# In a step whose product begins a half, the piece goes ahead of the product; the first transposition of x moves one step later

## The chip, the cores and the metric

The kernel runs on one core of a Trainium2 chip. The metric is the device time of one execution in microseconds (us); lower is better. The core has five engines that work side by side: PE (TensorE, matrix products, results into the accumulation memory PSUM), DVE (VectorE), ACT (ScalarE), POOL (GpSimd) and SP (SyncE, which here only issues transfers). Each engine takes its own instructions in the order of its own queue and waits on semaphores for what others have to finish first.

## What is computed

The input is x with 16 graphs of 1024 nodes and 128 features, and one adjacency matrix of 1024 by 1024 for all of them. Three transformer layers with 8 heads of 16 features, masked by the adjacency, are followed by one graph attention layer. Cut to what matters (`ln` is the layer norm):

```
for l in 0, 1, 2:
    Q, K, V = x @ Wq, x @ Wk, x @ Wv                      # 8 heads of 16
    scores  = where(adj == 0, -inf, Q K^T / 4)            # 1024 x 1024 a head
    x = ln(x + softmax(scores) V @ Wo + bo)
    x = ln(x + relu(x @ W1 + b1) @ W2 + b2)               # 256 hidden
h   = x @ W
e   = leaky_relu(h @ a_src [:, None] + h @ a_dst [None, :], 0.2)
out = ln(softmax(where(adj == 0, -inf, e)) h + x)
```

## The kernel before

**Blocks, halves, steps.** `blocks` (L655) lists 48 pairs of a graph and a layer, four graphs at a time, so that the four take turns at layer 0, then at layer 1, then at layer 2. A block is 32 steps: two groups of four heads, two halves of 512 queries (`qh`), and eight tiles of 128 keys (`kt`). A half is one group and one `qh`, so a block has four halves of eight steps. Below, "step 12" is the step with that number within its block, and its key tile is the rest of the number divided by 8.

**A step** (the loop at L768) issues three things, and PE and ACT run them in this written order (the schedule is manual for these two at L763; the order on DVE, POOL and SP is settled by the compiling framework, which looks ahead):

- `score_step` (L415): four matmuls make the scores of four heads, two by two into two PSUM tiles `s` of two banks each. There are three such tiles (`slot`, L130). Of each pair, either ACT takes the exponential and POOL multiplies with the mask (L430, L431: only the first pair, and not where `kt` is 2, 5 or 7), or DVE adds the mask and ACT takes the exponential a little later (L433, L445).
- `av_due` (L727): the product of the step four steps earlier (`AHEAD`). `av_step` (L447) multiplies its exponentials with the values, and adds into the one accumulator `sums`, a single PSUM bank (L719). After the eighth key tile of a half, `finish` (L453) has DVE transpose the accumulator into `tt` (L461), and POOL scales it. The next half's first product overwrites `sums`, so it waits for that transposition. With four steps of delay a half's product begins at steps 4, 12, 20 and 28.
- `piece` (L691): one task of the chains of other work that stand waiting, if one is due. Nearly every piece needs the one PSUM bank `t` (`bank`, L134: `bufs=1`): its matmuls write there, and ACT or DVE copies the result out before the next piece's matmuls may write.

**Pieces.** `proj_tasks` (L357) makes the next block's projections: `t0` transposes x (twice), `split` makes K and Q as a high and a low part (four pieces: ACT writes `hi`, L385, then DVE writes `lo`, L386), `v` makes the values (two pieces, ACT copies them out, L392). `post_tasks` (L469) does what comes after the attention of the block before: `both` (transpositions on DVE), `out_proj` (two pieces, out through DVE at L329 with statistics behind it), `x1t` (two), `ffn1` (four, out through ACT at L506), `ffn2` (two). `last_tasks` (L541) is the graph attention layer of a graph: `xt`, `nodes`, `rows_gh`, `edges`, `two` (edges of one quarter and `aggregate` of the quarter before), `end`. The `edges` also need two tiles `s` and one of the six tiles `e` that the steps use.

**When a piece is due.** The table `AT` (L34) gives the step, within its block, for each of the pieces of `proj` and `post`; those of `last` keep a gap after the piece before them. Each step takes at most one piece, from the first chain that has one due. In a block without the last layer the pieces stand thus: `t0` at 3 and 6, `split` at 9, 11, 14 and 17, `v` at 19 and 20, `both` at 8 or 10, `out_proj` at 12 and 22, `x1t` at 23 and 25, `ffn1` at 26, 27, 28 and 30, `ffn2` at 0 and 8 of the block after. Twelve blocks (three groups of four) also carry the last layer of an earlier graph, and nearly every step of theirs has a piece; the last group's follows in the final block and behind it (`AT_END`, L35).

Of the kernel before, what the change touches and what calls it, by code (L numbers as in the profile page):

```python
# [30 lines left out]
FIRST = 1  # L31


AT = {"proj": (3, 6, 9, 11, 14, 17, 19, 20), "post": (12, 22, 23, 25, 26, 27, 28, 30, 32, 40, 41)}  # L34
AT_END = {3: (12, 21, 22, 24, 25, 26, 27, 28, 30, 31), 2: (8, 9, 13, 14, 15, 16, 17, 18, 20, 21)}  # L35
AHEAD = 4
BOTH_ON_DVE = (2, 5, 7)
# [78 lines left out]
def fast_path(ctx: ExitStack, tc: tile.TileContext, a: dict, out: bass.AP, flag):  # L116
# [108 lines left out]
    def first_weights():  # L225
        W[0].update(load_layer(nc, nc.sync, const, a, 0, ("Wo", "b2", "W1", "b1", "W2", "ln1_g", "ln2_g")))
        norm_weights(nc.sync, 0)
# [173 lines left out]
    def stack(m, g):  # L401

        for pp in range(2):
            for n, order in (("Wk", (0, 1, 0, 1)), ("Wq", (0, 0, 1, 1))):
                t = work.tile([P, N], F32R, tag=n, name=n, bufs=4)
                r0 = (g * J + 2 * pp) * HD
                for i, part in enumerate(order):
                    behind["stack"] = nc.sync.dma_start(t[i:P:4, :].bitcast(F32), state[n, m][part][r0:r0 + 2 * HD, :].bitcast(F32)).ins
                state[n, g, pp] = t
# [37 lines left out]
    def av_step(step, e, acc, first, last):  # L447
        m, g, qh, kt = step
        for j in range(J):
            nc.tensor.matmul(acc[j * SLOT:j * SLOT + HD + 1, :], v_bufs[m % 2][:, kt, 2 * j + g, :], e[:, j, :],  # L450
                             start=first, stop=last)

    def finish(g, qh, acc):  # L453

        def run():
            if g == 0 and qh == 0:
                state["A"] = work.tile([P, 2, 16, G, HD], F32, tag="A", name="A", bufs=1)
                state["recs"] = work.tile([P, G, 2, 16], F32, tag="recs", name="recs", bufs=2)
            tt = work.tile([P, 16, SLOT], F32, tag="tt", name="tt", bufs=1)
            with soon():  # L460
                nc.vector.transpose(tt.rearrange("p a b -> p (a b)"), acc)  # L461
            rec = state["recs"][:, g, qh, :]
            nc.vector.reciprocal(rec, tt[:, :, HD])
            nc.gpsimd.tensor_mul(state["A"][:, qh, :, g, :], tt[:, :, :HD],
                                 rec[:, :, None].to_broadcast([P, 16, HD]))
        return run
# [195 lines left out]
    def put(tasks, mark, chain=None, first=False, table=None):  # L662

        if chain is None:
            chain = {"due": now[0], "queue": deque()}
            chains.insert(0 if first else len(chains), chain)
        for n, task in enumerate(tasks):
            at = now[0] // (4 * NT) * 4 * NT + (table or AT[mark[0]])[n] if mark[0] in AT else None
            chain["queue"].append(task + (mark if n == len(tasks) - 1 else None, at))
        return chain  # L670

    def take(chain):

        _, f, tiles, mark, _ = chain["queue"][0]
        if any(free[t[1:]] == 0 for t in tiles.split() if t[0] == "+"):
            return False
        chain["queue"].popleft()
        f()
        for t in tiles.split():
            free[t[1:]] += -1 if t[0] == "+" else 1  # L680
        done.add(mark)
        chain["due"] = now[0]
        if not chain["queue"]:
            chains.remove(chain)
        return True

    def is_due(chain):
        gap, at = chain["queue"][0][0], chain["queue"][0][4]
        return now[0] >= (chain["due"] + gap if at is None else at)

    def piece():  # L691
        for chain in chains:
            if is_due(chain) and take(chain):
                return

    def need(mark):
        while mark not in done:
            first = next(c for c in chains if any(q[3] == mark for q in c["queue"]))
            assert take(first) or any(take(c) for c in list(chains) if c is not first)
# [22 lines left out]
    waiting = deque()  # L722
# [4 lines left out]
    def av_due(n):  # L727

        for item in [w for w in waiting if w[2] <= n]:
            step, e, _ = item  # L730
            half = step[:3]
            if half not in accs:
                if accs:
                    continue
                accs[half] = sums
                left[half] = NT
            waiting.remove(item)
            left[half] -= 1
            av_step(step, e, accs[half], left[half] == NT - 1, left[half] == 0)
            if left[half]:  # L740
                continue
            m, g, qh = half
            b, l = blocks[m]
            while g == 0 and qh == 0 and last_attn:
                need(last_attn.pop())
            finish(g, qh, accs.pop(half))()
            if m == len(blocks) - 1:
                if g == G - 1:
                    if qh == 0:
                        final.append(post_tasks(b, l)[1])  # L750
                    put(final[0][qh], ("final", qh), first=True)
                    if qh == 1:
                        put(last_tasks(b), ("last", b), chains[0])
            elif g == G - 1 and qh == 1:
                post = post_tasks(b, l)[0]
                chain = put(post[:1], ("attn", b, l))
                put(post[1:], ("post", b, l), chain, table=AT_END.get(len(blocks) - m))
                last_attn.append(("attn", b, l))
                if l == L - 1:
                    put(last_tasks(b), ("last", b), chain)  # L760

    n = 0
    with tc.manual_schedule(engines={mybir.EngineType.PE, mybir.EngineType.Activation}):  # L763
        for m, (b, l) in enumerate(blocks):
            order = [(g, qh) for g in range(G) for qh in range(2)]
            if m in (0, len(blocks) - 1):
                order.sort(key=lambda x: x[1])
            for at, (g, qh, kt) in enumerate((g, qh, kt) for g, qh in order for kt in range(NT)):  # L768
                now[0] = n
                if at == (6 if m == 0 else 1):  # L770
                    stack(m, 1)
                if n == 6:
                    with tc.issue_after(behind["stack"]):
                        first_weights()
                        other_weights()
                if n == 20:
                    with tc.issue_after(behind["pool"]):
                        biases()
                if n == 40:
                    with tc.issue_after(behind["dve"]):  # L780
                        last_weights()
                if at == 0 and m + 2 < len(blocks) and blocks[m + 2][1] == 0:
                    put([(0, fetch(blocks[m + 2][0]), "+x")], ("fetch", blocks[m + 2][0]))
                if m + 1 < len(blocks):
                    if at == (6 if m == 0 else 0):
                        need(("post",) + (blocks[m + 1][0], blocks[m + 1][1] - 1) if blocks[m + 1][1] else
                             ("fetch", blocks[m + 1][0]))
                        put(proj_tasks(m + 1), ("proj", m + 1), first=True)
                    if at == (24 if m == 0 else 21):
                        need(("proj", m + 1))  # L790
                        stack(m + 1, 0)
                step = m, g, qh, kt
                if FIRST <= n < FIRST + 4:

                    with tc.manual_schedule(engines={mybir.EngineType.DVE}):
                        e = score_step(step)
                        neighbours(4 + n - FIRST)
                        masks(4 + n - FIRST, mask_rows(4 + n - FIRST))
                else:
                    e = score_step(step)  # L800
                waiting.append((step, e, n + AHEAD))
                av_due(n)
                piece()
                n += 1
        exponentials(0)
        for n in range(n, n + 2 * AHEAD):
            now[0] = n
            av_due(n)
            piece()
        tail[0] = True  # L810
        while chains:
            now[0] += 1
            for chain in list(chains):
                if is_due(chain):
                    take(chain)
# [236 lines left out]
```

## Time and profile before

Median of three runs: 3982.8 us (3978.19 to 3985.26). The profiled execution took 3983.09 us, its span in the trace is 3981.2 us: 1.9 us lie around it.

| engine | busy us | share of the span |
|---|---|---|
| PE | 3758.5 | 94% |
| DVE | 3408.3 | 86% |
| ACT | 3392.8 | 85% |
| POOL | 3331.4 | 84% |
| weight loads (beside PE) | 1558.5 | 39% |

The busy time by stretch, one stretch a block, tells two kinds of blocks:

| stretch (us from the start) | what it is | length | PE busy | DVE | ACT | POOL |
|---|---|---|---|---|---|---|
| 466.0 to 539.3 | a block without the last layer | 73.3 | 70.82 | 65.33 | 69.42 | 64.73 |
| 836.1 to 931.7 | first block with it | 95.6 | 90.32 | 82.32 | 72.25 | 77.83 |
| 931.7 to 1028.7 | second | 97.0 | 90.52 | 80.97 | 72.49 | 76.88 |
| 1028.7 to 1127.5 | third | 98.8 | 91.77 | 81.42 | 73.28 | 78.53 |
| 1127.5 to 1221.1 | fourth | 93.6 | 90.84 | 79.10 | 70.85 | 75.64 |
| 1221.1 to 1294.2 | without it again | 73.1 | 70.63 | 65.08 | 69.22 | 64.58 |

To read it: PE works all but 2.5 us of 73 in the first kind and all but 3 to 7 us in the second. The other engines have some slack each, but they have it in places, not everywhere: an average of 86% can hold stretches where an engine is the last to be ready.

### The profile page before, as it was taken

Reading aid. Unit: us, or ns where it says so; the run is one execution under the profiler, and the core shown is the slowest. Engines: PE = TensorE matmul, PEld = TensorE weight load, DVE = VectorE, ACT = ScalarE, POOL = GpSimd, SP = SyncE. Lnnn points to the kernel's source line nnn. Section 1 sums busy time; section 2 is a strip of 40 time slices with the busy share of each in tenths; the row PEclk is TensorE's granted clock in tenths of the full one; section 3 lists DMA queues with packets and bytes.
Section 4 is the critical chain, followed back from the end, with each engine's and each line's share of the span. In section 5 each row is a group of like instructions: output and inputs, shape, how many; then the busy total and the mean of one; then the engine's idle time right before and its main releaser. Section 6 shows DMA issues by size and latency. Waiting matters only on the chain.

```text
span 3981.2 us, 107823 instructions
## 1 busy us (share of the span) xinstructions
PE 3758.5 (94%) x44501; PEld 1558.5 (39%) x44501; DVE 3408.3 (86%) x5326; ACT 3392.8 (85%) x3961; POOL 3331.4 (84%) x3010
## 2 busy tenths in 40 slices
PE   7999999999999999999999999999999999999996
PEld 2333333344443333334444333333444433333345
DVE  7888988988888988988888898888888898898874
ACT  7999999977779999997777999999777799999860
POOL 4788888987789888988778888888877898898875
PEclk8999999999999999999999999999999999999998
DMA  6222222112222222222222222221222212222200
GB/s 163 65 65 53 55 65 63 46 48 65 56 58 57 65 65 54 54 65 55 55 55 55 65 53 56 65 64 45 55 55 55 71 46 62 65 51 58 66 8 20
DMA packets 124465, 233.13 MB, mean 59 GB/s; under 512 B 34624, under 2 KB 73792, under 8 KB 123968
## 3 DMA queue, kind: packets, MB, share of 16 engines
q1 hardware_dynamic: 123056, 225.74, 22.5%
q8 instruction: 354, 5.80, 0.6%
q14 instruction: 143, 1.17, 0.1%
q10 hardware_dynamic: 912, 0.42, 0.0%
HBM read 15.54 MB, written 8.39 MB: 6 GB/s over the span
## 4 chain that ended last, share of the span: by engine, by line
PE 61%; DVE 22%; POOL 9%; ACT 4%; issue 3%; SPq 0%; DMA 0%; DVEq 0%; ACTq 0%; POOLq 0%
PE acc L450 23%; PE t L297 19%; PE s L423 16%; DVE e L433 13%; POOL e L431 3%; POOL x L341 2%; PE t L286 2%; DVE lo L386 2%; DVE st L322 2%; ACT e L445 2%; ACT e L430 2%; DVE tt L461 1%; POOL mv L339 1%; PE s L297 1%; POOL x L345 1%
## 5 line engine op out<-in xcount | busy, mean ns | idle before, releaser
L433 DVE TENSOR_TENSOR e<-s,mask_add 128x1024 f32<-128x1024 f32 x2112 | 2493.6, 1213 | 344.6 <-PE s L423 263.7
L445 ACT ACTIVATE e<-e 128x1024 f32<-128x1024 f32 x2112 | 2203.4, 1060 | 206.1 <-DVE e L433 187.9
L431 POOL TENSOR_TENSOR e<-e,mask 128x1024 f32<-128x1024 f32 x960 | 1933.5, 2026 | 419.0 <-ACT e L430 419.0
L450 PE MATMUL acc<-e,v 128*17 128x512 f32 x12288 | 1627.8, 601 | 73.3 <-DVE tt L461 47.8
L423 PE MATMUL s<-Wq,Wk 64*128 64x512 f32 x6144 | 1185.0, 456 | 58.1 <-DVE e L433 41.3
L430 ACT ACTIVATE e<-s 128x1024 f32<-128x1024 f32 x960 | 980.8, 1022 | 227.5 <-PE s L423 226.5
L423 PEld LDWEIGHTS s<-Wq,Wk 64*128 64x128 f32 x6144 | 501.2, 185 | 1027.9 <-DVE e L433 417.1
L450 PEld LDWEIGHTS acc<-e,v 128*17 128x17 f32 x12288 | 208.6, 95 | 582.1 <-issue 452.0
L341 POOL TENSOR_SCALAR x<-x,mv 128x128 f32<-128x128 f32 x896 | 389.1, 447 | 23.5
L345 POOL TENSOR_TENSOR x<-x,ln_g 128x1024 f32<-128x1024 f32 (+1 forms) x97 | 229.5, 2367 | 25.1 <-PE t L286 22.6
L339 POOL TENSOR_TENSOR mv<-mv,half_neg 128x4 f32<-128x4 f32 x224 | 232.4, 1038 | 18.6
L297 PE MATMUL t<-hd,e 128*32 128x129 f32 x7040 | 208.2, 275 | 1.2
L329 DVE TENSOR_TENSOR x<-t,x 128x512 f32<-128x512 f32 x191 | 130.8, 685 | 86.9 <-PE t L297 86.9
L297 PEld LDWEIGHTS t<-hd,e 128*32 128x32 f32 x7040 | 194.6, 110 | 16.0 <-issue 5.0
L322 DVE BATCH_NORM_STATS2 st<-x 128x6 f32<-128x128 f32 x896 | 197.3, 280 | 3.3
L297 PE MATMUL t<-x1T,W 128*32 128x512 f32 x1520 | 198.0, 592 | 0.0
L297 PEld LDWEIGHTS t<-W,hT 128*32 128x32 f32 x6080 | 170.0, 110 | 58.5 <-issue 45.5
L297 PE MATMUL t<-W,hT 128*32 128x128 f32 x6080 | 183.4, 273 | 0.2 <-DVE x L625 0.2
L286 PE MATMUL t<-identf,x 128*128 128x128 f32 x872 | 151.0, 289 | 34.0 <-DVE lo L386 15.4
L286 PEld LDWEIGHTS t<-identf,x 128*128 128x128 f32 x872 | 92.9, 141 | 230.2 <-issue 108.3
L337 POOL TENSOR_SCALAR mv<-mv 128x4 f32<-128x4 f32 x224 | 53.0, 236 | 124.6 <-DVE mv L324 98.8
L610 DVE SCALAR_TENSOR_TENSOR e<-s,mask 128x1024 f32<-128x1024 f32 x128 | 150.3, 1214 | 5.9 <-PE s L607 5.0
(118 smaller groups left out, 2573.9 us busy)
## 6 DMA issues: line engine op xcount, KB each, us to landing
Wk<-hi SPq DMA_DIRECT2D x384, 128.0 KB
Wk<-lo SPq DMA_DIRECT2D x384, 128.0 KB
Wq<-hi SPq DMA_DIRECT2D x384, 128.0 KB
Wq<-lo SPq DMA_DIRECT2D x384, 128.0 KB
x<-in_x_dram SPq DMA_DIRECT2D x16, 512.0 KB
out_dram<-x SPq DMA_DIRECT2D x31, 256.0 KB
ai<-in_adj_dram SPq DMA_DIRECT2D x8, 512.0 KB
g_rows<-parts SPq DMA_DIRECT2D x124, 4.0 KB
```

The costliest lines, as they stand in the source:

```text
L286: nc.tensor.transpose(ps[:, t * P:(t + 1) * P], src[:, 4 * h + t, :], identf)
L297: nc.tensor.matmul(dst[j:j + SLOT, :], lhsT[:, j:j + SLOT], rhs, start=start, stop=stop)
L322: nc.vector.bn_stats(st[:, t, :], z[:, t, :])
L339: nc.gpsimd.tensor_tensor(v, v, half_neg[:, ts], OP.pow)
L341: nc.gpsimd.tensor_scalar(z[:, t, :], z[:, t, :], mv[:, t, 0:1], mv[:, t, 1:2], op0=OP.add, op1=OP.mult)
L345: nc.gpsimd.tensor_mul(z, z, rows(gain, n))
L423: nc.tensor.matmul(ps[:, r * 512:(r + 1) * 512], k[64 * r:64 * r + 64, kt * P:(kt + 1) * P], q[64 * r:64 * r + 64, q0:q0 + 512], start=Tru ...
L430: nc.scalar.activation(ev, psv, AF.Exp, scale=HD ** -0.5)
L431: behind["pool"] = nc.gpsimd.tensor_mul(ev, ev, m).ins
L433: behind["dve"] = nc.vector.tensor_add(ev, psv, m).ins
L445: nc.scalar.activation(ev, ev, AF.Exp, scale=HD ** -0.5)
L450: nc.tensor.matmul(acc[j * SLOT:j * SLOT + HD + 1, :], v_bufs[m % 2][:, kt, 2 * j + g, :], e[:, j, :], start=first, stop=last)
```

## The change

In a step in which the product that is due begins a half (its key tile is 0, and it is the first in the waiting list), the piece is issued before the product and not after it. And the first entry of `AT["proj"]`, the step of `t0` for the first half of x, goes from 3 to 4.

```diff
-AT = {"proj": (3, 6, 9, 11, 14, 17, 19, 20), ...
+AT = {"proj": (4, 6, 9, 11, 14, 17, 19, 20), ...
...
                 waiting.append((step, e, n + AHEAD))
+                begins = waiting[0][2] <= n and waiting[0][0][3] == 0
+                if begins:
+                    piece()
                 av_due(n)
-                piece()
+                if not begins:
+                    piece()
                 n += 1
```

No instruction is added or taken away: 3060 on POOL, 4462 on ACT, 29958 on PE, 6546 on DVE and 1928 on SP in both programs. At steps 4, 12, 20 and 28 PE's order goes from scores, product, piece to scores, piece, product, wherever the step has a piece.

## Prediction

> **What bounds the kernel now.** I read the engines' busy time first, then the waits, then the timeline around the four steps that the change touches. PE is at 94% of the span, and the groups show where its idle time ahead of matmuls lies:
>
> ```profile
> PE 3758.5 (94%) x44501; PEld 1558.5 (39%) x44501; DVE 3408.3 (86%) x5326; ACT 3392.8 (85%) x3961; POOL 3331.4 (84%) x3010
> ...
> L450 PE MATMUL acc<-e,v 128*17 128x512 f32 x12288 | 1627.8, 601 | 73.3 <-DVE tt L461 47.8
> ```
>
> The reader should see that PE idles 73.3 us ahead of the product, 47.8 us of it until DVE has transposed the accumulator (84 of 192 times). That is what the change can win, about 48 us or 1.2%. Whether it does is read from the steps. This is step 12 of a block without the last layer (times from the span's start, then duration):
>
> ```profile
> 492.82 1.04 PE L297 MATMUL t<-xT,Wk 128*32 128x512 f32 x8
> ...
> 493.79 0.73 PE L423 MATMUL s<-Wq,Wk 64*128 64x512 f32 x4
> 494.24 0.70 DVE L461 STREAM_TRANSPOSE tt<-acc 128x512 f32<-128x512 f32 x1
> 494.31 0.58 ACT L385 CAST hi<-t 128x512 fp32r<-128x512 f32 x1
> ...
> 494.92 0.69 DVE L386 TENSOR_TENSOR lo<-t,hi 128x512 fp32r<-128x512 f32 x1
> ...
> 495.09 1.05 PE L450 MATMUL acc<-e,v 128*17 128x512 f32 x8 [0.57 <-DVE tt L461]
> ...
> 495.94 1.07 PE L297 MATMUL t<-Wo,aT 128*32 128x128 f32 x32
> ...
> 496.94 0.73 PE L423 MATMUL s<-Wq,Wk 64*128 64x512 f32 x4
> ```
>
> The gap of 0.57 is the prize. But beside it the bank `t`, filled by the `split` of step 11, is copied out only until 494.92 + 0.69 = 495.61, later than `tt`, which ends at 494.94. The piece of step 12 (`Wo`) writes that bank. Now it starts at 495.94, behind the product, and finds it free. The same at step 28, where no gap stands before the product at all:
>
> ```profile
> 530.22 1.04 PE L297 MATMUL t<-x1T,W 128*32 128x512 f32 x8
> ...
> 531.19 0.73 PE L423 MATMUL s<-Wq,Wk 64*128 64x512 f32 x4
> ...
> 531.56 0.71 ACT L506 ACTIVATE hT<-t,b 128x512 f32<-128x512 f32 x1
> ...
> 531.85 1.05 PE L450 MATMUL acc<-e,v 128*17 128x512 f32 x8
> ...
> 532.72 1.04 PE L297 MATMUL t<-x1T,W 128*32 128x512 f32 x8
> ```
>
> and at step 20, where the copy-out of `v` ends at 512.52 + 0.58 = 513.10 and `tt` at 513.09:
>
> ```profile
> 512.39 0.70 DVE L461 STREAM_TRANSPOSE tt<-acc 128x512 f32<-128x512 f32 x1
> 512.52 0.58 ACT L392 COPY v<-t 128x512 f32<-128x512 f32 x1
> ...
> 513.24 1.05 PE L450 MATMUL acc<-e,v 128*17 128x512 f32 x8 [0.55 <-DVE tt L461]
> ```
>
> **What the Trainium skill says.** "PSUM — Partial Sum Buffer", section "Engine vs sequencer instructions": matmuls start and complete in program order, and the queues of the other engines are strictly first in, first out. So a piece that waits for its bank holds the product behind it, even if that is ready. The same page, "PSUM bank collisions raise a hardware error": accesses of two engines to one bank and quadrant must be kept apart by semaphores, so the piece must wait for the copy-out. The trace agrees: at steps 12 and 20 the first product starts 0.15 us after `tt` ends, and by the list of waits the weight loads of pieces wait 48.0 us in all for `lo` (129 times) even now. "Perfetto Trace Analysis", "Identifying Performance Opportunities", says that the same gap repeating can mean too little PSUM for the next tile; here it is the one accumulator bank, 0.57 in block after block, and one bank `t` beside it.
>
> **The change, part by part.** Orders and waits in the changed program: in a block without the last layer DVE's order changes in one place (statistics of `Wo` ahead of one mask addition), POOL's and ACT's in one each at step 4; the `Wo` piece of step 12 waits for the DVE subtraction of step 11, `v` of step 20 for ACT's copy, `ffn1` of step 28 for ACT's relu. No DMA moves there: `t0` issues none. Spacings of PE from the lines above: product to piece 0.85 to 0.87, product to scores 0.99 (477.14 to 478.13 at step 4 of this block), DVE's or ACT's end to a waiting matmul 0.15; piece to product is not in the trace of before, both use column tiles, and I take 0.86 as for product to piece (at most 1.0, the piece to scores).
>
> - Step 12: `Wo` starts at 495.61 + 0.15 = 495.76, the product at 496.62, the next scores at 497.61. Before: 496.94. Loss 0.67. What was hidden, the wait for `lo`, lay under the product (1.05 us); that cover is gone.
> - Step 20: `v` at 513.10 + 0.15 = 513.25, where the product stood before. The two change places: 0.0 (up to 0.1).
> - Step 28: `ffn1` at 531.56 + 0.71 + 0.15 = 532.42, product 533.28, scores 534.27. Before: 533.69. Loss 0.58.
> - Step 4 with `t0` moved: before, `t0` and the scores lay between the last product and the first; after, the scores and `t0`. Equal cover. `tt` ends at 476.29 + 0.71 = 477.00 whatever PE does, since DVE works on a mask addition until then; the second scores pair waits for ACT's exponential until 476.12, so scores end at 476.65 and the product starts at about 477.17 instead of 477.14. Loss 0.03. Without the move `t0` would have stood at step 3 and nothing at 4.
>
> Sum 1.28 a block. Can the rest of the block absorb it? After step 12 DVE works without a pause until about 507, but ACT does too from step 14 on, and both wait for scores that are now late; going through steps 13 to 18 with these durations I find 0.55 to 0.7 still there at step 18. After step 28 DVE has about 1 us free a step, PE none, so all of it stays. I take 1.2 a block. 34 blocks have `split` at 11 and `Wo` at 12: 34 x 1.2 = 41 us, bounds 20 and 50.
>
> The twelve blocks with the last layer differ, as every step is filled there. The chain of `last` is moved a step later, its row copies, the loads of x and the stores on SP and the normalisations on POOL with it; each has a step or more before its use, so I put them at nothing; if that cover is gone, a step, 2.5 us, in a block. What stands on the path:
>
> - Step 12: `two` now comes there, right after the scores. Its second `edges` tile waits for the exponential of step 12, 0.35. In the changed program DVE's masking of the edges waits for the end of the aggregation, since their `e` tile comes free only then, where before 2 x 1.2 us of it ran beside its 3.75 us. Behind it stand one mask addition (1.2) and then the two operations that free `t`, so `Wo` waits about 1.75 at step 13. Together about 2.5 (bounds 0.5 and 4).
> - Step 4: `ffn2` comes a step nearer. `tt` stands behind its copy-out, statistics and one addition, 0.75 + 1.05 + 1.2 + 0.7 = 3.7 after its end, and PE has 1.3 us of work in that time instead of 2.9: 1.5 more of a wait in the third and fourth block of a group, 0.9 in the second, 0 in the first.
> - Step 20: 0.45 in the second and third, where no gap stood before. Step 28: 0.5 to 0.85.
>
> By block 3.0, 4.7, 5.3 and 4.6, together 17.6, three times 53 us. These blocks hold 3 to 7 us of other waits that some of it falls into, and DVE catches up; I keep 0.7 of it, 37 us (bounds 5 and 60). The final block and its tail: 1.
>
> Sum on the profiled execution: 3983.1 + 41 + 37 + 1 = 4062 us. It lies 0.3 us above the median, so the same holds for that.
>
> **Rivals.**
>
> - A, faster: the bank is free in time, and the pieces fill the gaps. For it: 47.8 us of waits on `tt`. Against it: `lo` ends 1.1 us after the scores at step 12, ACT's relu 0.35 us after them at 28. It decides only if these copy-outs moved ahead of the scores' end. Price: the gaps, 3983 - 48 = 3935. 3%.
> - B, the ordinary blocks lose, those with the last layer come out even, since the later pieces sit no worse than before: 3983 + 41 = 4024. 20%.
> - C, the loss in ordinary blocks is taken up by the later waits on DVE (0.59 at step 3, 0.2 at 17 and 25), 0.3 a block stays, and the twelve lose half: 3983 + 10 + 19 = 4012. Against it: these waits start from a piece of PE's own and move with it. 9%.
> - D, the twelve lose all of the 53 and an addition waits for a late `e` tile besides: 3983 + 45 + 75 = 4103. 13%.
> - E, no difference beyond 0.2%, which is about what a measurement of this kernel can tell: gains at step 12 and 20 balance losses at 28. 2%.
>
> **How the numbers follow.** The forecast has 53%, with its own range of 4040 to 4085. The range for 8 in 10 reaches into B and D: 4012 to 4098. Faster by over 0.2% has 3% (A), within 0.2% 2% (E), slower 95%.
>
> **What would show it.** Right: waits of PE's `t` groups on DVE `lo`, on ACT `hT` and on ACT `v` grow to about 1.1, 0.75 and 0.6 us each in 34 blocks, while the wait of the product on `tt` falls from 47.8 us to almost nothing; ordinary blocks last about 74.3 instead of 73.1 us, the others about 100 instead of 97. Wrong: ordinary blocks of 73 us or less, or `Wo` starting before `lo` has ended.

## The result and the profile after

The changed kernel takes 4123.54 us (median of five runs, 4116.39 to 4124.21) against 3982.8: a ratio of 1.0352, with an interval of 1.0338 to 1.0366. It is slower, as forecast, but by 141 us and not by 79: outside the range. The profiled execution took 4124.21 us, its span is 4122.4 us.

The page of the changed kernel, busy time of the engines and the product's group:

```profile
PE 3805.0 (92%) x44501; PEld 1559.9 (38%) x44501; DVE 3408.9 (83%) x5326; ACT 3391.8 (82%) x3961; POOL 3335.6 (81%) x3010
...
L450 PE MATMUL acc<-e,v 128*17 128x512 f32 x12288 | 1633.1, 604 | 29.4 <-POOL e L431 25.6
```

The other engines do what they did. PE is busy 46.5 us longer with the same 44501 matmuls, which no step of the prediction has. The product's idle time fell from 73.3 to 29.4 us, and DVE's `tt` is no longer its first releaser: the prize was collected. The list of waits of the changed kernel (engine, waiting line, what it waits for: us in total, times, longest) shows what it cost:

```profile
PEld t L297 <- DVE lo L386: 79.1, 109, 1.6
PE t L297 <- DVE lo L386: 71.5, 62, 2.0
...
PEld t L297 <- ACT hT L506: 54.7, 113, 0.8
...
DVE e L610 <- PE t L297: 38.9, 13, 3.6
...
PE acc L450 <- POOL e L431: 25.6, 21, 2.7
...
PE t L297 <- ACT v L392: 14.5, 31, 0.5
PE t L297 <- ACT hT L506: 11.6, 30, 0.4
...
PE acc L450 <- DVE tt L461: 3.8, 5, 1.0
```

The same two waits for `lo` in the kernel before:

```profile
PE t L286 <- DVE lo L386: 15.4, 19, 0.9
...
PE t L297 <- DVE lo L386: 3.5, 4, 0.9
```

The wait for `tt` went from 47.8 to 3.8 us. Against that the matmuls of pieces at L297 wait 71.5 us for `lo` (3.5 before; with the transpositions at L286 it is 77.5 against 18.9), and 26 us for the two copies of ACT, for which none waited before. Each of these is a piece that waits for its bank `t`. Step 12 of the same block as in the prediction, PE and DVE of the changed kernel (start, duration):

```profile
501.31 0.73 PE L423 MATMUL s<-Wq,Wk 64*128 64x512 f32 x4
501.77 0.71 DVE L461 STREAM_TRANSPOSE tt<-acc 128x512 f32<-128x512 f32 x1
501.90 0.57 ACT L385 CAST hi<-t 128x512 fp32r<-128x512 f32 x1
...
502.51 0.69 DVE L386 TENSOR_TENSOR lo<-t,hi 128x512 fp32r<-128x512 f32 x1
...
503.25 1.08 PE L297 MATMUL t<-Wo,aT 128*32 128x128 f32 x32 [1.21 <-DVE lo L386]
...
504.15 1.04 PE L450 MATMUL acc<-e,v 128*17 128x512 f32 x8
...
505.12 0.73 PE L423 MATMUL s<-Wq,Wk 64*128 64x512 f32 x4
```

`tt` ends at 502.48, so the product could have started at about 502.63. It stands behind `Wo`, which waits for `lo` until 503.25. At step 28 it is the relu of ACT, at step 20 its copy of `v`:

```profile
521.39 1.08 PE L297 MATMUL t<-Wv,xT 128*32 128x128 f32 x32 [0.46 <-ACT v L392]
...
540.49 1.06 PE L297 MATMUL t<-x1T,W 128*32 128x512 f32 x8 [0.39 <-ACT hT L506]
541.38 1.04 PE L450 MATMUL acc<-e,v 128*17 128x512 f32 x8
542.35 0.73 PE L423 MATMUL s<-Wq,Wk 64*128 64x512 f32 x4
```

An ordinary block (without the last layer) now lasts 74.3 us, 1.14 more. The busy time by stretch (length, then each engine's busy time with its number of instructions, the granted clock, DMA share, GB/s), one row for that ordinary block and four for the first group of blocks with the last layer; the kernel before:

```profile
466.10:539.30 73.20, 70.72 (x724) 25.92 (x720) 65.23 (x97) 69.32 (x79) 64.63 (x57) 1.00 0.23 59
836.10:931.70 95.60, 90.32 (x1333) 44.21 (x1329) 82.32 (x141) 72.25 (x91) 77.83 (x76) 1.00 0.23 57
931.70:1028.70 97.00, 90.52 (x1333) 44.41 (x1329) 80.97 (x140) 72.49 (x91) 76.88 (x75) 1.00 0.22 56
1028.70:1127.50 98.80, 91.77 (x1341) 44.55 (x1337) 81.42 (x140) 73.28 (x92) 78.53 (x76) 0.98 0.22 56
1127.50:1221.10 93.60, 90.84 (x1284) 42.41 (x1280) 79.10 (x134) 70.85 (x81) 75.64 (x75) 0.98 0.23 58
```

and the changed one:

```profile
473.60:547.90 74.30, 70.85 (x724) 25.75 (x720) 65.26 (x97) 69.19 (x79) 64.76 (x57) 1.00 0.24 58
849.50:950.70 101.20, 91.57 (x1325) 43.93 (x1321) 81.80 (x141) 72.14 (x90) 76.17 (x75) 0.98 0.21 54
950.70:1054.30 103.60, 93.04 (x1333) 44.65 (x1329) 81.06 (x140) 72.45 (x91) 77.85 (x76) 0.98 0.21 53
1054.30:1160.40 106.10, 95.22 (x1341) 45.33 (x1337) 81.30 (x140) 72.99 (x92) 78.69 (x76) 0.97 0.20 52
1160.40:1267.20 106.80, 96.27 (x1292) 43.38 (x1288) 78.96 (x134) 71.97 (x82) 77.90 (x75) 0.95 0.20 51
```

The four gained 5.6, 6.6, 7.3 and 13.2 us, and the granted clock in them fell to 0.95 in the last. Over the whole run, from the first scores of each block to those of the next (the last part ends with PE's last matmul):

| part | before | after | difference |
|---|---|---|---|
| twelve blocks with the last layer | 1158.2 | 1254.5 | +96.3 |
| the other 35 up to the final one | 2586.9 | 2627.8 | +40.9 |
| final block and what follows it | 206.4 | 210.0 | +3.6 |

Of the 96.3 us, 62.2 are PE idle and 34.2 PE busy longer with the same instructions. By step 19 the four blocks are 5.0, 3.6, 4.4 and 6.5 us behind, 19.5 of their 32.7; the rest comes after it, half of that in the fourth block.

### The profile page after: what moved, and what is told of

The parts are those of the page before. It is cut to its first block, busy times and chain, and to the rows that moved or that the text cites. A ratio compares the mean times of both kernels' runs of the same rounds, so it can differ in the third digit from the quotient of the medians.

```text
span 4122.4 us, 107829 instructions
## 1 busy us (share of the span) xinstructions
PE 3805.0 (92%) x44501; PEld 1559.9 (38%) x44501; DVE 3408.9 (83%) x5326; ACT 3391.8 (82%) x3961; POOL 3335.6 (81%) x3010
## 5 line engine op out<-in xcount | busy, mean ns | idle before, releaser
L450 PE MATMUL acc<-e,v 128*17 128x512 f32 x12288 | 1633.1, 604 | 29.4 <-POOL e L431 25.6
L423 PE MATMUL s<-Wq,Wk 64*128 64x512 f32 x6144 | 1195.1, 457 | 68.2 <-DVE e L433 48.4
L450 PEld LDWEIGHTS acc<-e,v 128*17 128x17 f32 x12288 | 217.5, 96 | 500.0 <-issue 414.1
L297 PE MATMUL t<-hd,e 128*32 128x129 f32 x7040 | 208.3, 275 | 10.8 <-DVE lo L386 9.9
L297 PE MATMUL t<-x1T,W 128*32 128x512 f32 x1520 | 201.8, 603 | 12.6 <-ACT hT L506 11.6
L297 PEld LDWEIGHTS t<-hd,e 128*32 128x32 f32 x7040 | 193.6, 110 | 28.8 <-issue 21.1
L297 PE MATMUL t<-W,hT 128*32 128x128 f32 x6080 | 186.5, 275 | 17.3 <-DVE lo L386 17.2
L297 PEld LDWEIGHTS t<-W,hT 128*32 128x32 f32 x6080 | 171.3, 111 | 79.3 <-issue 73.3
L286 PE MATMUL t<-identf,x 128*128 128x128 f32 x872 | 159.4, 296 | 40.0 <-POOL x L341 16.4
L286 PEld LDWEIGHTS t<-identf,x 128*128 128x128 f32 x872 | 95.8, 143 | 215.4 <-POOL x L341 70.0
```

Of the source, the lines that this page charges most:

```text
L286: nc.tensor.transpose(ps[:, t * P:(t + 1) * P], src[:, 4 * h + t, :], identf)
L297: nc.tensor.matmul(dst[j:j + SLOT, :], lhsT[:, j:j + SLOT], rhs, start=start, stop=stop)
L423: nc.tensor.matmul(ps[:, r * 512:(r + 1) * 512], k[64 * r:64 * r + 64, kt * P:(kt + 1) * P], q[64 * r:64 * r + 64, q0:q0 + 512], start=Tru ...
```

## The experiments

Two questions: is bank `t` the cause in ordinary blocks, and what costs 96 us in the twelve, where 37 were forecast? All edits are against the kernel before or the changed one, as said. Block sums of the profiled runs come first in a table (us; "ordinary" is one block):

| run | median | ordinary | twelve | others | last part |
|---|---|---|---|---|---|
| before | 3982.8 | 73.15 | 1158.2 | 2586.9 | 206.4 |
| after | 4123.5 | 74.29 | 1254.5 | 2627.8 | 210.0 |
| only the move of `t0` | 4085.4 | 73.76 | 1241.7 | 2609.3 | 207.2 |
| only the order | 4039.1 | 74.21 | 1174.8 | 2623.8 | 210.3 |
| both, in ordinary blocks only | 4022.8 | 74.29 | 1159.0 | 2626.3 | 207.4 |
| both, `t0` stays at 3 in the twelve | 4041.4 | 74.28 | 1174.3 | 2625.7 | 209.9 |
| both, `edges` a step earlier | 4061.3 | 74.28 | 1195.1 | 2627.8 | 208.4 |
| other bank, ordinary blocks | 3954.3 | 72.21 | 1156.8 | 2558.8 | 205.8 |

**The two parts alone.** Against before:

```diff
-AT = {"proj": (3, 6, ...
+AT = {"proj": (4, 6, ...
```

> Only the first transposition of x goes from step 3 to step 4; the piece stays behind the product. Theory 1 (in the twelve blocks with the last layer the loss comes from that move, since it pushes the whole chain of the last layer one step later): the twelve lose 3 to 6 us each, ordinary blocks about 0.45 (the product at step 4 waits for the transposition of the accumulator without t0 in front of it), in all about 3983 + 15 + 55 = 4053 us. Theory 2 (the loss in the twelve comes from the order, `two` ahead of the product at step 12): the twelve come out even, 3983 + 15 = 3998 us.

Measured: 4085.44 us, ratio 1.0266 (1.0234 to 1.0297), more than either theory had. The twelve lose 83.5 us by the move alone. Ordinary blocks lose 0.6 us, since `t0` then stands behind the waiting product instead of ahead of it. The other part is the new order with `t0` back at 3:

> Only the order: the piece ahead of the product that begins a half; t0 stays at step 3. Theory 1: ordinary blocks lose 1.2 us (0.67 at step 12, 0.58 at step 28), the twelve about 2 each, in all 3983 + 41 + 24 = 4048 us. Theory 2 (the order itself costs the twelve 8 us each, whatever stands at the steps): 3983 + 41 + 98 = 4122 us.

Measured: 4039.12 us, 1.0149 (1.0120 to 1.0179). The order alone gives the ordinary blocks nearly their whole loss (74.21 of 74.29) and the twelve only 16.6. So the two causes can be told apart: the order makes nearly all of the ordinary blocks' loss, the move of `t0` most of the twelve's (alone, the two cost the twelve 100 us together, and 96 in the changed kernel).

**The change by kind of block.** The changed kernel, with the condition that the block does not carry the last layer on both edits, and then with `t0` alone at 3 in the twelve:

```diff
+                carries = m > 10 and m % 12 in (11, 0, 1, 2)
-                begins = waiting[0][2] <= n and waiting[0][0][3] == 0
+                begins = waiting[0][2] <= n and waiting[0][0][3] == 0 and not carries
...
-                        put(proj_tasks(m + 1), ("proj", m + 1), first=True)
+                        put(proj_tasks(m + 1), ("proj", m + 1), first=True,
+                            table=(3 if carries else 4,) + AT["proj"][1:])
```

> The whole change, but only in blocks that do not carry the last layer. If the losses of the two kinds of blocks are independent: ordinary blocks 74.3 us as in the changed kernel, the twelve 95.6 to 99 us as before, in all 3983 + 40 = 4023 us. If a part of the loss of the twelve is carried over from the block before: 4040 us or more.

> The whole change, but t0 stays at step 3 in the twelve blocks that carry the last layer, so that their chain is not pushed. Theory 1: the twelve lose about 2 us each instead of 8, in all 3983 + 40 + 24 = 4047 us. Theory 2: they lose 8 each all the same, 4120 us.

Measured: 4022.82 us, 1.0108 (1.0079 to 1.0138), and 4041.44 us, 1.0155 (1.0126 to 1.0185). The first leaves the twelve as before (1159.0) and costs what the ordinary blocks lost, 39 us of them in the 35 others. The second gives the twelve 1174.3 instead of 1254.5: 80 us hang on one entry of a table, in twelve blocks.

**Why the move costs so much.** Step 3 was `t0`'s, step 4 that of `edges(0)` from the chain of the last layer, which keeps a gap after its piece before (in the first block of a group it is the first `two` that stands there). With `t0` at 4 in front, `edges(0)` comes at 5, and since every later piece of that chain keeps its gap, the chain is later up to its end. It is not one step only: in the second to fourth block the next `two` comes at 8 instead of 7, and as the `split` of step 11 goes ahead of the one after that, the next two stand at 12 and 15 instead of 10 and 13. The `ffn2` that had step 8 no longer stands ahead of the `split` of step 9 but behind it, at 10, and `end` comes at 22 instead of 21. The test gives `edges(0)` the step that `t0` left free, in the changed kernel:

```diff
-                (2, rows_gh, ""), (8, edges(0), ""), ...
+                (2, rows_gh, ""), (7, edges(0), ""), ...
```

> The changed kernel, with the gap ahead of edges(0) cut from 8 to 7, so that edges takes step 3 of its block, which t0 has left free, and the rest of the chain of the last layer stands where it stood in the kernel before or a step earlier. Theory T (the twelve blocks lose some 80 us because t0 at step 4 pushes the chain of the last layer a step later): the twelve come out near those of the run with the new order alone, 1165 to 1190 us instead of 1254.5, the whole at 4030 to 4060. Rival U (it is t0's own place at step 4, with the scores and ffn2 around it, that costs): the twelve stay above 1230, the whole at 4100 or more.

Measured: 4061.26 us, 1.0201 (1.0184 to 1.0218); the twelve at 1195.1. So 59 of the 80 us come back without touching `t0`: the chain's place is most of the cost. It is not all. The second block of each group stayed at 104 us (97 to 98 before). The trace shows that its chain did not come back to its old place: `edges(0)` stands at step 2, `two` at 5 and 8, so that `ffn2` is again at 10, behind the `split`, and `two` at 12. Of the loss, 4.6 us are there by step 11 and 7.0 by step 14; what each of these places costs was not tried. The theory's upper bounds, 1190 for the twelve and 4060 in all, were missed by 5 and 1 us.

**What the late chain runs into.** In the fourth block of the first group `ffn2` stands at step 10 behind a `split`; the trace of the changed kernel:

```profile
1192.91 1.05 PE L450 MATMUL acc<-e,v 128*17 128x512 f32 x8
1195.95 1.95 PE L297 MATMUL t<-W,hT 128*32 128x128 f32 x64 [2.00 <-DVE lo L386]
1197.84 0.73 PE L423 MATMUL s<-Wq,Wk 64*128 64x512 f32 x4
```

2.00 us for `lo`; in the kernel before, PE's matmuls wait for it 23 times in the whole run (the two lines above), 0.9 us at the longest. In the second block POOL is late. Its timeline from the changed kernel, then PE's:

```profile
1031.45 2.39 POOL L345 TENSOR_TENSOR x<-x,ln_g 128x1024 f32<-128x1024 f32 x1
1033.91 2.37 POOL L346 TENSOR_TENSOR x<-x,ln_b_last 128x1024 f32<-128x1024 f32 x1
1036.25 5.94 POOL L431 TENSOR_TENSOR e<-e,mask 128x1024 f32<-128x1024 f32 x3
```

```profile
1034.84 0.73 PE L423 MATMUL s<-Wq,Wk 64*128 64x512 f32 x4
1038.32 1.86 PE L450 MATMUL acc<-e,v 128*17 128x512 f32 x8 [2.74 <-POOL e L431]
1039.93 1.95 PE L297 MATMUL t<-Wo,aT 128*32 128x128 f32 x32
1041.81 0.73 PE L423 MATMUL s<-Wq,Wk 64*128 64x512 f32 x4
1042.47 1.05 PE L450 MATMUL acc<-e,v 128*17 128x512 f32 x8
```

Gain and bias of a whole x (4.8 us) stand ahead of a step's mask, and the product waits 2.74 us for it. What follows is the surprise: the next product takes 1.86 us instead of 1.05, and `Wo` 1.95 instead of 1.07. That is a part of PE's longer busy time; the last section says how much at most. To see how much POOL has in it, both kernels ran without gain and bias in `xt` and `end`, so these two operations on POOL are left out of the computation:

```diff
-                    scale_shift(state["x", b], w["ln2_g"], ln2_b_last)
+                    pass
...
-                scale_shift(y[:, 4 * h:4 * h + 4, :], wl["ln_gamma"], wl["ln_beta"])
```

> The changed kernel without the gain and bias that POOL applies behind xt and end (the second norm of layer 2 and the last norm are left without them). To be set against the kernel before without the same operations. Theory P (in the twelve blocks most of the loss is POOL's: the later chain puts these operations just ahead of normalisations and mask multiplications that PE waits for): the difference of the two is 60 to 85 us instead of 141, the waits of x1t on POOL and of the product on POOL in steps 24 to 26 are gone. Theory D (it is DVE and the bank t, at steps 8 to 18): the difference stays at 120 to 140 us.

> The kernel before without the same operations (left out: the gain and bias of the second norm of layer 2 and of the last norm). Its twelve blocks lose their waits on POOL at steps 23 and 24 (1.62 and 0.84 us): 15 to 30 us faster than the kernel before, 3950 to 3965 us, under both theories.

Measured: 4079.22 us for the changed one, 3961.3 for the one before. The change costs 117.9 us without that POOL work instead of 140.7, the twelve 78.9 instead of 96.3. POOL's part is thus about 20 us in all (23 by the medians of two runs each, 19 by the profiled runs) and 17 in the twelve. The larger part stays: 117.9 lies between the two expectations, just below the 120 of theory D. In the fourth block of the first group, 11.6 us of loss are left, and 7.4 of them are there by step 19, so in the steps in which the trace shows the waits for bank `t` and for DVE.

**Is it the bank?** The new order in ordinary blocks, `t0` at 3, and the piece that goes ahead of a product writes one of the score tiles `s` instead of bank `t`:

```diff
-        if head[0] or tail[0]:
+        if head[0] or tail[0] or ahead[0]:
             return slot()[:, :512]
...
+                begins = waiting[0][2] <= n and waiting[0][0][3] == 0 and not carries
                 if begins:
+                    ahead[0] = True
                     piece()
+                    ahead[0] = False
...
```

> The order of the change in ordinary blocks alone, t0 at step 3 everywhere, and the piece that goes ahead writes one of the three score tiles and not the bank t. If the wait for the copy-out of the bank t is what makes ordinary blocks slower: 73.1 - 1.0 = about 72.1 us a block instead of 74.3, in all about 3980 - 34 = 3946 us. If it is the order itself (the product later, its buffers free later): 74.2 us a block, 4020 us. If the score tiles become short: 4000 us or more.

Measured: 3954.31 us, 0.9933 (0.9916 to 0.9949): faster than both kernels. Ordinary blocks take 72.21 us, 0.94 less than before and 2.00 less than with the order alone (74.21), from which they differ by the bank. Its step 12:

```profile
490.65 0.73 PE L423 MATMUL s<-Wq,Wk 64*128 64x512 f32 x4
491.31 1.08 PE L297 MATMUL s<-Wo,aT 128*32 128x128 f32 x32
492.21 1.04 PE L450 MATMUL acc<-e,v 128*17 128x512 f32 x8
493.18 1.08 PE L423 MATMUL s<-Wq,Wk 64*128 64x512 f32 x4
```

`Wo` starts 0.66 us after the scores and fills the gap; `lo` is still being written then (DVE, 491.78 for 0.69). So the idea of the order was sound, and the one bank spoiled it. The old order with the other bank was not run. In the kernel before, the same `Wo` found the bank free (it began 0.33 us after the end of `lo`), so at this step another bank alone has no wait to take away. With `t0` at 4 in ordinary blocks besides:

> The run in which the piece ahead of the product writes a score tile, with t0 at step 4 in the blocks without the last layer (in the others t0 stays at 3 and the old order stays). Theory T: with another bank a piece at step 4 covers the wait for tt there as it does at 12 and 20, so ordinary blocks come to 71.7 to 72.2 us, the whole to 3935 to 3955. Rival: t0 at step 4 holds the score tile that the next step's scores need, and ordinary blocks are at 72.4 or more, the whole at 3960 or more.

Measured: 3954.39 us, 0.9932 (0.9915 to 0.9948), ordinary blocks 72.29. The same time; the block is between the two bounds, so neither expectation holds, and a piece at step 4 is worth nothing here.

**A miss: another way to the gap.** If `tt` is late, let its source end sooner: in the kernel before, the product that ends a half goes ahead of the scores of its step.

```diff
+                ends = waiting and waiting[0][2] <= n and waiting[0][0][3] == NT - 1
+                if ends:
+                    av_due(n)
```

> The kernel before, and one other edit: in a step whose product ends a half, the product goes ahead of the scores, so that the scores, the piece and the next scores all lie between it and the product that begins the next half; no piece changes its place among the pieces. If the wait for the transposition is all that is lost there and the bank t is left alone: the gaps of about 0.57, 0.55 and 0.24 us at steps 12, 20 and 4 go, 1.3 us a block, about 3980 - 50 = 3930 us. If DVE, which gets the last scores of a half later, is then what PE waits for: 3975 to 4000 us.

Measured: 4008.80 us, 1.0069 (1.0052 to 1.0086), slower than each expectation. The gap is gone (idle ahead of products 17.4 us, none of it for `tt`). But the same bank takes its place, as the list of waits shows:

```profile
PE t L297 <- DVE lo L386: 64.3, 50, 1.4
```

It was 3.5 us before. In an ordinary block this kernel is 0.14 us ahead of the kernel before when step 12 begins and 0.85 us behind when step 13 begins; at the end 0.29 are left. The step between, from the same block as above:

```profile
494.62 1.06 PE L297 MATMUL t<-xT,Wk 128*32 128x512 f32 x8
...
495.62 0.73 PE L423 MATMUL s<-Wq,Wk 64*128 64x512 f32 x4
496.28 1.05 PE L450 MATMUL acc<-e,v 128*17 128x512 f32 x8
...
496.86 1.16 DVE L433 TENSOR_TENSOR e<-s,mask_add 128x1024 f32<-128x1024 f32 x1
...
497.94 0.67 DVE L386 TENSOR_TENSOR lo<-t,hi 128x512 fp32r<-128x512 f32 x1
...
498.76 1.08 PE L297 MATMUL t<-Wo,aT 128*32 128x128 f32 x32 [1.42 <-DVE lo L386]
```

The scores and the `split` of step 11 stand behind one product more, DVE comes to `lo` only after a mask addition of step 12, and `Wo` waits 1.42 us for the bank. So PE does wait for DVE, as the second expectation had it, but for the same buffer as in the change itself.

## Why the prediction was right in kind and too small

- Step 12, `Wo` waits for `lo`, 0.67: right. The next scores are 0.65 us later in the block. Step 20, nothing: right, the loss even shrinks by 0.08 there, though `v` waits 0.46. Step 28, 0.58: it adds 0.47. Step 4, 0.03: 0.04. Together 1.14 a block where the sum had 1.28 and 1.2 were taken; "34 x 1.2 = 41 us" against 40.9 measured. At step 28 the sum's 0.15 us from the end of a copy-out to the matmul that waits for it was too much: `ffn1` starts 0.05 us after the relu there, `Wo` 0.05 us after `lo` at step 12. The rest of the block takes up next to nothing, as said. That bank `t` is the cause is shown by the run with the other bank.
- The final block and tail: 3.6 instead of 1.
- The twelve blocks: "I keep 0.7 of it, 37 us (bounds 5 and 60)" against 96.3. This is the step that failed. It priced four steps of each block, with the moved chain in them, and these were not too low: at 12 it had 2.5, and in the second block of the first group steps 12 and 13 take 6.68 and 4.50 us where in the kernel before a step with `two` takes 6.18 and one with `Wo` 2.65, together 2.35 more; at 20 it had 0.45, measured 0.13. (The order alone, with the chain in its old place, costs the twelve 16.6 us.) What it put at nothing is the chain at its other steps: "The chain of `last` is moved a step later, its row copies, the loads of x and the stores on SP and the normalisations on POOL with it; each has a step or more before its use, so I put them at nothing". That cover was counted against the use of each result, not against what each piece meets in PE's order at its new step: `ffn2` behind a `split`, the masks of steps behind gain and bias on POOL. Nor did it have the half clock that followed the longer of these pauses. The bound named for a lost cover, "a step, 2.5 us, in a block", would have been 30 us; the runs show about 80 (the changed kernel against the one with `t0` at 3 in the twelve), of which 59 come back when `edges` takes step 3.
- Rival D had the direction, that the twelve lose all; at 75 us for them it was too low as well. Rival B, that the twelve come out even, is what the run with the change in ordinary blocks alone gives (4022.8 for 4024), but not what the change does. Rival A names the condition under which its gain comes, that the bank is free in time; with another bank 28 of the 48 us were got.
- Of the sum's three terms two were right within 3 us; the third is short by 59, nearly the whole error of 61.
- The signs named ahead: `tt` to almost nothing (3.8), ordinary blocks about 74.3 (74.29), the others about 100 (104.5 on average, wrong). Waits on `lo` of about 1.1 (1.21 at step 12) hold, those on `hT` and `v` were put at 0.75 and 0.6, and PE's idle time there is 0.39 and 0.46.

## What to carry to other kernels

A piece that is moved ahead of a waiting product fills its gap only if the buffer that it writes is free sooner than the product's own input; look at the release of the buffer first, and give the piece another one if there is one. Where pieces keep gaps to their forerunners, moving one entry moves a whole chain: list every instruction at its new step, and price what it now stands behind on each engine, not only when its result is used. A closed gap is no gain by itself: the gap on `tt` was closed in two ways at a loss, and both times a piece then waited longer for its one bank; with a second bank the first way gained.

## What the runs showed of the hardware

A pause of PE can cost more than itself. After the pause of 2.74 us above, and after another of 2.98 us before an `x1T` piece in the fourth block, products take 1.86 to 1.91 us instead of 1.05. The granted clock by stretch of the changed kernel, around the two places:

```profile
1032.00:1036.00 4.00, 3.57 (x48) 1.43 (x40) 2.90 (x5) 4.00 (x9) 3.92 (x2) 1.00 0.44 131
1036.00:1042.00 6.00, 3.69 (x42) 2.03 (x44) 2.47 (x4) 1.74 (x2) 6.00 (x4) 0.72 0.01 3
...
1248.00:1260.00 12.00, 10.19 (x52) 3.06 (x56) 4.71 (x6) 6.43 (x8) 11.43 (x10) 0.72 0.01 1
```

Half the clock for x of 6.0 us gives a mean of 0.72 with x = 0.28 x 6.0 / 0.5 = 3.4 us, and in the 12 us twice as much: windows of one length. The trace's records of the clock say the same, pieces of 3.41 us at half rate that all begin at one phase of a grid of 3.41 us. The Trainium skill, "TensorE: Matmul & The Clock Gate", Part 1, section "What's actually happening", gives the same: a free-running window of 3413 ns, and either half or full rate. Its section "HAM oscillation — how this bites in real kernels" warns of idle gaps of more than about 3.4 us; here less was enough, and the measurement decides.

How much was enough can be read when PE's idle time is summed over each window of that grid, in the changed kernel between 0.2 and 3.6 ms. Ten windows without matmuls of `edges` hold 2.0 us of idle time or more (2.00 to 3.08), and half rate begins in the window after every one of them; after those with 1.76 us or less it never begins. So it matters how a pause lies in the grid: the 2.00 us before `ffn2` in the fourth block of the first group fell on two windows, 1.48 us in the fuller one, and no half rate followed. Nine more times half rate begins after a window in which matmuls of `edges` ran, with 1.26 to 1.50 us of idle time, and all ten times of the kernel before are of this kind (0.72 to 1.51 us); why so little was enough there is not shown.

In all, the records show 10 such windows at half rate before (34.1 us) and 22 after (75.1 us; three of the ten spells after a pause last two windows). At half rate the 41 us more are worth at most 20 us of work: an estimate, from these figures, of this effect's part in the 96 us and in the 34.2 us that PE is busy longer there. The rest of the longer busy time stays open, and no run took the clock alone. With the order alone, which costs the twelve 16.6 us, the windows make 23.9 us; with the move of `t0` alone, which costs them 83.5, 75.1 as in the changed kernel.
